# Reordering TensorE's products in a gated attention block: like divisions of the array side by side

## The chip, the core and the metric

The kernel runs on one core of one Trainium2 chip. Its time is the device time in microseconds (us) of one launch; the median of several runs is compared. All data are float32.

## What is computed

Two residual blocks over x (32 items of 256 tokens, 256 wide), cut to what matters:

```python
def _L0_xattn_ref(q, k, v, ...):        # k = v = ctx, 77 rows an item; H, D = 8, 128
    f_q, f_k, f_v = proj(q), proj(k), proj(v)   # layer_norm(t) @ w_in.T, split into 8 heads
    cosine_sim = einsum('hqnd,hqmd->hqnm', f_q, f_k) / (qn * kn)
    var_component = einsum('hqn,hqm->hqnm', q_ratio, k_ratio)
    cov_component = cosine_sim * decorr_scale       # one number a head, from all of f_q
    mixed = cw * cosine_sim + vw * cov_component + ww * var_component
    out = einsum('hqnm,hqmd->hqnd', mixed, f_v)
    return out_heads_side_by_side @ w_out.T + b_out

def _L0_ffn_ref(x, Wq, Wk, Wv, Wo, Wff):        # 16 heads of 16
    q, k, v = split_heads(x @ Wq), split_heads(x @ Wk), split_heads(x @ Wv)
    scores = einsum('bqd,bkd->bkq', q, k) / sqrt(256)
    z = einsum('bkq,bkv->bqv', softmax(scores, -1), v)
    z = l2_normalize(l2_normalize(z @ Wo) @ Wff)
    return gelu(z, approximate=False)

x = x + tanh(g_xattn) * _L0_xattn_ref(_layernorm(x), ctx, ctx, ...)
x = x + tanh(g_ffn) * _L0_ffn_ref(_layernorm(x), ...)
```

## The kernel before

A prologue (to about 150 us) loads and transposes the weights, gathers what the decorrelation scale needs from all tokens, and starts the first items. Then a software pipeline runs. Its unit is an item (256 tokens, two tiles of 128), and its order is written out by hand: the list `cycle` (line 1151) holds pairs of "how many items ahead" and a stage, and the loop at line 1216 runs through the list once a round, for n from -4 to 32. A round so holds stages of several items: the scores of item n, the output of item n-1, the attention of item n+1, the query features of n+2, the key features of n+3.

Each engine is wrapped in `InOrder` (line 22): its instructions stay in the order in which the stages issue them. So an instruction that waits holds up everything behind it on its engine. Semaphores between engines are set by the framework.

[...]Pool `ps` (line 71) has three tiles of one bank, called mm, which all products except two use: scores take two tiles of two banks (`ps_s`), the mix of values one bank (`ps_z`). A new mm tile goes to the bank that comes free first in the framework's planning; the product that writes it waits until the last reader of the bank's old tile is done.

TensorE's products differ in how they divide its 128 x 128 array:

- the whole array: query_features and key_features (`winT`, 512 columns of data), attend (`vw`,`s`), ff_project and ff_values, ff_out (`w_of`,`zT`), transpose_keys, the query ratios (`qrp`), and the transpositions against `ident` (xn, fq, xf);
- halves of 64 columns: `paired` (line 310), used by key_outputs and query_scores for pairs 0 and 1; two products side by side;
- quarters of 32 columns: pair 2 of key_outputs and query_scores, and mix_values (`zp`); four side by side;
- quarters of 32 rows: scores (`sc`).

A score unit u (0 to 3 in an item) is this chain: scores (line 491) makes four products on TensorE and two maxima on VectorE (`nm`, 1.2 us each); exponents (line 512), in two halves of four activations on ScalarE, with sums; scale_values (line 524) on VectorE takes the reciprocal of the sums and multiplies v into `vz`; mix_values (line 537) multiplies `vz` with the exponents on TensorE into `zp`. After unit 3, VectorE copies zp to `zT`.

ff_out (line 557) makes the two products of zT with `w_of`; ScalarE squares one half of the bank and VectorE copies the other to `u` after it. scale_queries (line 383) takes statistics of fq on VectorE, a power and the scaling of fq by `rq` on GpSimd. transpose_queries (line 398) transposes fq into `fqT`, copied out by ScalarE or VectorE. ff_add (line 602) adds u to x on VectorE and issues the output's DMA from SP. norm_inputs (line 194) makes `xn` on GpSimd; transpose_inputs (line 205) transposes it, and ScalarE copies it out with scale and bias as `xTc`. Every instruction is recorded under line 30, so the profile's groups are told apart by tile names.

Of the kernel before, what the change touches and what calls it, by code (L numbers as in the profile page):

```python
# [8 lines left out]
F32 = mybir.dt.float32  # L9
AF = mybir.ActivationFunctionType  # L10
ALU = mybir.AluOpType
# [3 lines left out]
P = 128  # L15
# [18 lines left out]
def gated_block_kernel(  # L34
# [25 lines left out]
    B, S, D = x.shape  # L60
    M = cx.shape[1]
    NT = S // P
# [6 lines left out]
    pa = ctx.enter_context(tc.tile_pool(name="pa", bufs=2))  # L69
# [6 lines left out]
    pe, act, dve, pool = (  # L76
        InOrder(tc, e) for e in (nc.tensor, nc.scalar, nc.vector, nc.gpsimd)
    )
# [8 lines left out]
    ident = const.tile([P, P], F32, name="ident")  # L87
# [11 lines left out]
    gcol = const.tile([P, 2], F32, name="gcol")  # L99
    bcol = const.tile([P, 2], F32, name="bcol")  # L100
# [36 lines left out]
    def mm_tile():  # L137
        return ps.tile([P, 512], F32, tag="mm", name="mm")
# [20 lines left out]
    def transpose_in(src):  # L159

        pt = mm_tile()
        for t in range(NT):
            for c in range(2):
                pe.transpose(
                    pt[:, c * S + t * P : c * S + (t + 1) * P],
                    src[:, t, c * P : (c + 1) * P],
                    ident,
                )
        return pt
# [6 lines left out]
    kept = [{} for _ in range(B)]  # L176
    given = set()

    def run(b, stage, *which):
        key = (b, stage.__name__, which)  # L180
        if key not in given:
            given.add(key)
            stage(b, *which)
# [21 lines left out]
    def transpose_inputs(b):  # L205
        k = kept[b]
        pt = transpose_in(k["xn"])
        xT = pa.tile([P, 2, S], F32, tag="xTc", name="xTc", bufs=1)
        for c in range(2):
            act.activation(  # L210
                xT[:, c, :], pt[:, c * S : (c + 1) * S], AF.Identity,
                bias=bcol[:, c : c + 1], scale=gcol[:, c : c + 1],
            )
        k["xTc"] = xT

# [94 lines left out]
    def paired(pt, k, pair, rhs):  # L310

        for c in range(2):
            for i in range(2):
                h = 4 * pair + 2 * c + i
                pe.matmul(
                    pt[MA * i : MA * (i + 1), c * S : (c + 1) * S],
                    lhsT=k["fvT"][:, h, 0:MA], rhs=rhs[:, h, :], start=True, stop=True,
                )

    def key_outputs(b, pair):  # L320


        k = kept[b]
        if pair == 0:
            k["vw"] = pa.tile([P, 5, D], F32, tag="vw", name="vw", bufs=2)
        pg = mm_tile()
        if pair < 2:
            paired(pg, k, pair, woutT)
            out = k["vw"][:, 2 * pair : 2 * pair + 2, :].rearrange("p g c -> p (g c)")
            (act.copy if pair == 0 else dve.tensor_copy)(out, pg)  # L330
            return
        for i in (1, 0):
            for j in range(4):
                n = 32 if i else MR + 1
                pe.matmul(
                    pg[32 * j : 32 * j + n, 0:D], lhsT=k["fvT"][:, 2 * j + i, MA : MA + n],
                    rhs=woutT[:, 2 * j + i, :], start=(i == 1), stop=(i == 0),
                )
        dve.tensor_tensor(k["vw"][:, 4, :], pg[:, 0:D], bias_t, ALU.add)

    def query_scores(b, pair):

        k = kept[b]
        if pair == 0:
            k["s"] = pa.tile([P, 5, S], F32, tag="s", name="s", bufs=1)
        pg = mm_tile()
        if pair < 2:
            paired(pg, k, pair, k["fqT"])
            out = k["s"][:, 2 * pair : 2 * pair + 2, :].rearrange("p g q -> p (g q)")
            (act.copy if pair == 0 else dve.tensor_copy)(out, pg)  # L350
            return
        for t in range(NT):
            pe.matmul(
                pg[:, t * P : (t + 1) * P], lhsT=qrps[t].rearrange("p h w -> p (h w)"),
                rhs=ident, start=(t == 0), stop=False,
            )
        for i in range(2):
            for j in range(4):
                n = MR + 16 * i
                pe.matmul(  # L360
                    pg[32 * j : 32 * j + n, 0:S], lhsT=k["fvT"][:, 2 * j + i, MA : MA + n],
                    rhs=k["fqT"][:, 2 * j + i, :], start=False, stop=(i == 1),
                )
        act.copy(k["s"][:, 4, :], pg[:, 0:S])
# [33 lines left out]
    def transpose_queries(b, t, hh):  # L398
        k = kept[b]
        if (t, hh) == (0, 0):  # L400
            k["fqT"] = pa.tile([P, H, S], F32, tag="fqT", name="fqT", bufs=1)
        pt = mm_tile()
        for i in range(4):
            h = hh * 4 + i
            pe.transpose(
                pt[:, i * P : (i + 1) * P], k["fq", t][:, h * P : (h + 1) * P], ident
            )
        out = k["fqT"][:, hh * 4 : hh * 4 + 4, t * P : (t + 1) * P]
        src = pt.rearrange("p (h q) -> p h q", q=P)
        (dve.tensor_copy if hh == t else act.copy)(out, src)  # L410

    def attend(b, t):

# [441 lines left out]
    qrps, vzs = [], []  # L855
# [55 lines left out]
    for g in range(-2, NG):  # L911
# [9 lines left out]
        for i in range(4):  # L921
            k = 4 * g + i
# [29 lines left out]
    pt = mm_tile()  # L952
# [7 lines left out]
    for c in range(2):  # L960
        dve.scalar_tensor_tensor(
            gs[:, c, c * P : D], gram[:, c, 0 : D - c * P], gcol[:, c : c + 1],
            grow[:, c * P : D], ALU.mult, ALU.mult,
        )
    run(0, transpose_inputs)
    run(1, norm_inputs)
    pt = mm_tile()
    for c in range(2):
        pe.matmul(
            pt[:, c * D + c * P : (c + 1) * D], lhsT=lbT[:, c * P : (c + 1) * P],  # L970
            rhs=lbT[:, D + c * P : 2 * D], start=True, stop=True,
# [11 lines left out]
    pt = mm_tile()  # L983
# [3 lines left out]
    pt = mm_tile()  # L987
    for h in range(H):
        for c in range(2):
            pe.matmul(  # L990
                pt[:, 2 * h : 2 * h + 2],
                lhsT=winT[:, c, h * P : (h + 1) * P],
                rhs=qk[:, c, :],
                start=(c == 0),
                stop=(c == 1),
# [21 lines left out]
    pt = mm_tile()  # L1017
# [20 lines left out]
    pt = mm_tile()  # L1038
# [6 lines left out]
    def square_up(hh):  # L1045
# [26 lines left out]
    pt = mm_tile()  # L1072
# [12 lines left out]
    pt = mm_tile()  # L1085
# [2 lines left out]
    dve.tensor_copy(ds, pt[0:H, 0:1])  # L1088
    pool.tensor_tensor(ds, ds, phalf, ALU.pow)
    act.activation(ds, ds, AF.Exp, scale=-5.0 / (P * P))  # L1090
    run(0, key_features)
    run(0, measure_keys)
    run(0, align_keys)
# [6 lines left out]
    dve.tensor_scalar(dg[:, 0, :], ident[0:H, 0:H], hw[:, 0:1], None, ALU.mult)  # L1100

    dve.tensor_scalar(dg[:, 1, :], ident[0:H, 0:H], lg[:, 2:3], 4.0, ALU.mult, ALU.mult)
    run(0, scale_queries, 1)
    run(0, transpose_queries, 0, 0)
    run(0, transpose_queries, 0, 1)
    pt = mm_tile()
    pe.matmul(
        pt[:, 0 : 2 * H], lhsT=ones[0:H, :], rhs=dg.rearrange("p w h -> p (w h)"),
        start=True, stop=True,
# [2 lines left out]

    run(0, weigh_keys)
    run(0, scale_keys)
    run(1, transpose_inputs)
    run(1, query_features, 0, 0)
    run(1, query_features, 0, 1)
    run(0, transpose_queries, 1, 0)
    run(0, transpose_queries, 1, 1)
    run(0, transpose_keys, 0)  # L1120
    run(0, transpose_keys, 1)
    run(1, key_features)
    for pair in range(3):
        run(0, query_scores, pair)
    for pair in range(3):
        run(0, key_outputs, pair)
    run(1, measure_keys)
    run(1, align_keys)
    run(0, attend, 0)
# [20 lines left out]

    cycle = [
        (4, load_queries),
        (0, ff_project, "k"),
        (0, ff_project, "q"),
        (0, ff_values),
        (1, transpose_queries, 0, 0),
        (-1, mix_values, 3),
        (1, transpose_queries, 0, 1),
        (0, scores, 0),
        (1, transpose_queries, 1, 0),  # L1160
        (1, transpose_queries, 1, 1),
        (0, exponents, 0, 0),
        (-1, ff_out, 0),
        (1, query_scores, 0),
        (-1, ff_out, 1),
        (1, query_scores, 1),
        (0, exponents, 0, 1),
        (0, scale_values, 0),
        (1, query_scores, 2),
        (-1, ff_norm_first),  # L1170
        (0, scores, 1),
        (-1, ff_norm_second),
        (2, transpose_inputs),
        (0, mix_values, 0),
        (2, measure_keys),
        (2, align_keys),
        (0, exponents, 1, 0),
        (0, exponents, 1, 1),
        (2, query_features, 0, 0),
        (2, query_features, 0, 1),  # L1180
        (0, scale_values, 1),
        (3, key_features),
        (2, weigh_keys),
        (0, scores, 2),
        (0, mix_values, 1),
        (2, scale_keys),
        (0, exponents, 2, 0),
        (1, attend, 0),
        (1, ff_stats, 0),
        (2, scale_queries, 0),  # L1190
# [7 lines left out]
        (2, query_features, 1, 0),  # L1198
        (2, query_features, 1, 1),
        (1, ff_norm, 1),  # L1200
        (2, transpose_keys, 0),
        (2, transpose_keys, 1),
        (0, scores, 3),
        (0, mix_values, 2),
        (-1, ff_add),
        (2, key_outputs, 0),
        (1, ff_transpose),
        (0, exponents, 3, 0),
        (2, key_outputs, 1),
        (0, exponents, 3, 1),  # L1210
        (2, key_outputs, 2),
        (2, scale_queries, 1),
        (0, scale_values, 3),
        (3, norm_inputs),
    ]
    for n in range(-4, B + 1):
        for ahead, stage, *which in cycle:
# [36 lines left out]
```

## Time and profile before

| what | value |
|---|---|
| time, median of 3 runs (lowest to highest) | 1516.35 us (1516.2 to 1518.54) |
| the profiled execution's own time | 1517.04 us |
| its span, first to last instruction | 1515.1 us |
| TensorE's mean granted clock | 0.982 |
| busy: DVE (VectorE), ACT (ScalarE), POOL (GpSimd) | 1044.1, 982.8, 516.8 us |
| busy: PEld (TensorE's weight loads, beside its products) | 846.5 us |
| a round of the cycle, between two zT copies | 42.26 us, in five rounds 43.98 us |
| first and last zT copy of the 32 items | 202.64 and 1499.91 us |
| HBM traffic over the span | 21 GB/s |

The longest waits are those of GpSimd for VectorE and ScalarE (`rq` 295.5 us, `i` 290.6 us, `rs` 230.0 us in total), of the VectorE maxima for the scores (115.2 us) and of ScalarE's `vw` copy for the products (107.4 us). Idle time of an engine that isn't the bottleneck costs nothing by itself.

How to read it: one execution was taken by the profiler. PE is TensorE's matmul stream; its ends are modelled, so times between starts are more exact than durations. In a line of a timeline stand the start, the time from there to the end of the last instruction merged into the line, the engine, the source line, the operation, out<-in by tile names, the shapes, and in brackets the idle time before it with what ended it.

### The profile page before, as it was taken

To read this page: it belongs to the slowest core of one execution; us is meant where nothing else is said; L and a number is where in the kernel's file an instruction comes from. 1 tells how busy PE (TensorE), PEld (TensorE's weight loads), DVE (VectorE), ACT (ScalarE), POOL (GpSimd) and SP (SyncE) were. 2 spreads that over 40 slices of the span, in tenths; PEclk is the share of its full clock that TensorE was granted. 3 is DMA by queue.
4 is the path that set the end of the run, shared out by engine and by line. 5 is a ranking of instruction groups with operands and counts; after the bars stand their busy time and mean duration, and the time that the engine had idled before them with its cause. 6 is when DMAs were issued, how large, how long until landed. Compare 5 with 4: busy or idle time off the path is not lost.

```text
span 1515.1 us, 26525 instructions
## 1 busy us (share of the span) xinstructions
PE 1468.9 (97%) x9313; PEld 846.5 (56%) x9313; DVE 1044.1 (69%) x2989; ACT 982.8 (65%) x3102; POOL 516.8 (34%) x656
## 2 busy tenths in 40 slices
PE   6898999999999999999999999999999999999985
PEld 6755555555555555555555555555555555555541
DVE  5735677777677676777676776776786767777843
ACT  5622566766676766766676766766676766766665
POOL 5912333333323323333323333333323323333311
PEclk9989999999999999999999999999999999999996
DMA  7500000000000000000000000000000000000000
GB/s 263 166 15 26 9 10 24 20 26 18 29 24 6 18 23 23 23 24 21 27 18 9 22 23 23 23 18 29 24 20 13 15 23 16 17 13 11 8 8 14
DMA packets 26194, 43.31 MB, mean 29 GB/s; under 512 B 6010, under 2 KB 11055, under 8 KB 26062
## 3 DMA queue, kind: packets, MB, share of 16 engines
q1 hardware_dynamic: 25230, 41.63, 8.6%
q8 instruction: 73, 1.20, 0.3%
q14 instruction: 59, 0.48, 0.1%
q10 hardware_dynamic: 832, 0.00, 0.0%
HBM read 22.98 MB, written 8.39 MB: 21 GB/s over the span
## 4 chain that ended last, share of the span: by engine, by line
PE 91%; ACT 2%; DVE 1%; POOL 0%; issue 0%; ACTq 0%; POOLq 0%
PE mm L30 73%; PE sc L30 9%; PE zp L30 8%; ACT e L30 1%; DVE nm L30 0%; ACT L30 0%; ACT ge L30 0%; POOL i L30 0%; POOL nrx L30 0%; DVE vz L30 0%; ACT fc L30 0%; DVE x L30 0%; ACT xT L30 0%; ACT xTc L30 0%; ACT u L30 0%
## 5 line engine op out<-in xcount | busy, mean ns | idle before, releaser
L30 ACT ACTIVATE e<-sc,nm 128x256 f32<-128x256 f32 x1024 | 469.8, 486 | 65.9 <-DVE nm L30 61.5
L30 DVE TENSOR_REDUCE nm<-sc 128x4 f32<-128x1024 f32 x256 | 301.4, 1218 | 115.2 <-PE sc L30 115.2
L30 PE MATMUL mm<-winT,xTc 128*128 128x512 f32 x512 | 235.6, 602 | 1.1 <-ACT xTc L30 1.1
L30 ACT ACTIVATION_READ_ACCUMULATOR e<-sc,nm 128x1 f32 x1024 | 224.1, 219 | 0.0
L30 POOL TENSOR_TENSOR rq<-qt,nhalf 128x8 f32<-128x8 f32 x64 | 105.4, 1647 | 295.5 <-DVE qt L30 295.5
L30 PE MATMUL sc<-q,kTf 32*128 32x512 f32 x1024 | 154.4, 648 | 6.1 <-ACT e L30 6.1
L30 PEld LDWEIGHTS mm<-winT,xTc 128*128 128x128 f32 x512 | 95.1, 191 | 107.3 <-issue 77.5
L30 PE MATMUL mm<-vw,s 128*128 128x256 f32 x640 | 147.7, 386 | 0.0
L30 PE MATMUL zp<-e,vz 128*32 128x256 f32 x2048 | 140.5, 393 | 5.1 <-DVE vz L30 5.1
L30 PEld LDWEIGHTS mm<-vw,s 128*128 128x128 f32 x640 | 119.6, 191 | 29.1 <-issue 14.1
L30 PE MATMUL mm<-w_of,zT 128*128 128x512 f32 x256 | 125.5, 614 | 0.8 <-DVE zT L30 0.8
L30 POOL TENSOR_TENSOR fq<-fq,rq 128x1024 f32<-128x1024 f32 x64 | 121.4, 1897 | 5.0
L30 POOL TENSOR_SCALAR i<-nn 128x2 f32<-128x2 f32 x64 | 14.3, 223 | 290.6 <-ACT ge L30 290.6
L30 PEld LDWEIGHTS zp<-e,vz 128*32 128x32 f32 x2048 | 54.3, 110 | 91.9 <-issue 33.9
L30 DVE BATCH_NORM_STATS2 qst<-fq 128x6 f32<-128x128 f32 x512 | 103.9, 275 | 0.0
L30 PE MATMUL mm<-fqT,fvT 128*64 128x256 f32 (+2 forms) x1024 | 102.9, 386 | 0.9 <-DVE fqT L30 0.7
L30 PE MATMUL mm<-woutT,fvT 128*64 128x256 f32 (+2 forms) x1024 | 101.0, 388 | 0.0
L30 POOL TENSOR_SCALAR rs<-mv 128x1 f32<-128x1 f32 x64 | 15.8, 247 | 231.5 <-DVE mv L30 230.0
L30 DVE COPY u<-mm 128x256 f32<-128x256 f32 x64 | 27.2, 425 | 91.5 <-ACT ge L30 91.4
L30 DVE TENSOR_TENSOR vz<-v,sums 128x128 f32<-128x128 f32 x128 | 86.8, 678 | 4.4
L30 ACT COPY fqT<-mm 128x512 f32<-128x512 f32 x64 | 37.5, 586 | 80.5 <-PE mm L30 80.5
L30 ACT COPY vw<-mm 128x512 f32<-128x512 f32 x32 | 18.8, 586 | 107.4 <-PE mm L30 107.4
(203 smaller groups left out, 2482.9 us busy)
## 6 DMA issues: line engine op xcount, KB each, us to landing
x<-in_x_dram SPq DMA_DIRECT2D x64, 256.0 KB
out_dram<-x SPq DMA_DIRECT2D x32, 256.0 KB
fv<-fvx SPq DMA_DIRECT2D x13, 308.0 KB
ct<-in_ctx_dram SPq DMA_DIRECT2D x4, 512.0 KB
w_in_n<-in_L_xattn_w_in_dram SPq DMA_DIRECT2D x2, 512.0 KB
w_out_n<-in_L_xattn_w_out_dram SPq DMA_DIRECT2D x1, 1024.0 KB
ct<-in_ctx_dram SPq DMA_DIRECT2D x1, 384.0 KB
fv<-fvx SPq DMA_DIRECT2D x1, 304.0 KB
```

The costliest lines, as they stand in the source:

```text
L30: return lambda *args, **kw: self._tc.keep_in_program_order(method(*args, **kw))
```

## The change

The list `cycle` is put into another order, and with it the stages of the first items ahead of it. In the new list each score unit stands beside products with 32 or 64 columns: the last mix and scores 0; scores 1, query_scores and mix 0; scores 2 and mix 1; scores 3, mix 2 and key_outputs. Between these four clusters stand stretches of whole-array products and transpositions. Projections k, q, v of an item and the first half of its queries' transposition go to the end of the round before; ff_add goes to the end of the round; norm_inputs goes ahead of transpose_keys.

To allow this, the query ratios, which were the first part of query_scores pair 2, become a stage of their own, query_ratios, whose mm tile is kept until pair 2 adds to it. key_outputs makes its `vw` tile at whichever pair comes first. The copy of xTc goes from ScalarE to VectorE. The copies of fqT are divided by half of the heads and no longer by half and tile: ScalarE takes heads 0 to 3, VectorE 4 to 7. No product, transposition or copy is added or left out.

```diff
@@ transpose_inputs
         for c in range(2):
-            act.activation(
-                xT[:, c, :], pt[:, c * S : (c + 1) * S], AF.Identity,
-                bias=bcol[:, c : c + 1], scale=gcol[:, c : c + 1],
+            dve.tensor_scalar(
+                xT[:, c, :], pt[:, c * S : (c + 1) * S], gcol[:, c : c + 1],
+                bcol[:, c : c + 1], ALU.mult, ALU.add,
             )
@@ key_outputs
-        if pair == 0:
+        if "vw" not in k:
             k["vw"] = pa.tile([P, 5, D], F32, tag="vw", name="vw", bufs=2)
@@
+    def query_ratios(b):
+
+        k = kept[b]
+        k["s"] = pa.tile([P, 5, S], F32, tag="s", name="s", bufs=1)
+        k["pr"] = mm_tile()
+        for t in range(NT):
+            pe.matmul(
+                k["pr"][:, t * P : (t + 1) * P], lhsT=qrps[t].rearrange("p h w -> p (h w)"),
+                rhs=ident, start=(t == 0), stop=False,
+            )
+
@@ query_scores
-        if pair == 0:
-            k["s"] = pa.tile([P, 5, S], F32, tag="s", name="s", bufs=1)
-        pg = mm_tile()
         if pair < 2:
+            pg = mm_tile()
             paired(pg, k, pair, k["fqT"])
...
-        for t in range(NT):
-            pe.matmul(
-                pg[:, t * P : (t + 1) * P], lhsT=qrps[t].rearrange("p h w -> p (h w)"),
-                rhs=ident, start=(t == 0), stop=False,
-            )
+        pg = k.pop("pr")
@@ transpose_queries
-        (dve.tensor_copy if hh == t else act.copy)(out, src)
+        (dve.tensor_copy if hh else act.copy)(out, src)
```

The order of the first items: transpose_inputs of item 1 goes ahead of key_features of item 0; scale_queries of item 0, tile 1, goes behind its scale_keys; key_outputs goes ahead of the query scores, in the order 2, 0, 1. The cycle after the change:

```python
cycle = [
    (4, load_queries),
    (-1, mix_values, 3), (0, scores, 0),
    (2, transpose_inputs), (0, exponents, 0, 0), (-1, ff_out, 0), (-1, ff_out, 1),
    (0, exponents, 0, 1), (1, transpose_queries, 1, 0), (1, transpose_queries, 1, 1),
    (2, query_features, 0, 0), (1, query_ratios), (0, scale_values, 0),
    (-1, ff_norm_first), (-1, ff_norm_second),
    (0, scores, 1), (1, query_scores, 0), (0, exponents, 1, 0), (1, query_scores, 1),
    (1, query_scores, 2), (0, exponents, 1, 1), (0, mix_values, 0),
    (2, measure_keys), (2, align_keys), (2, query_features, 0, 1), (0, scale_values, 1),
    (3, key_features), (2, weigh_keys),
    (0, scores, 2), (0, exponents, 2, 0), (0, mix_values, 1),
    (2, scale_keys), (1, attend, 0), (1, ff_stats, 0), (2, scale_queries, 0),
    (1, attend, 1), (0, exponents, 2, 1), (-1, ff_gelu), (2, warm_exponentials),
    (1, ff_norm, 0), (1, ff_stats, 1), (0, scale_values, 2),
    (2, query_features, 1, 0), (2, query_features, 1, 1), (1, ff_norm, 1),
    (3, norm_inputs), (2, transpose_keys, 0), (2, transpose_keys, 1),
    (0, scores, 3), (0, mix_values, 2),
    (2, key_outputs, 2), (2, key_outputs, 0), (2, key_outputs, 1),
    (1, ff_transpose), (2, transpose_queries, 0, 0), (0, exponents, 3, 0),
    (2, transpose_queries, 0, 1), (2, scale_queries, 1),
    (1, ff_project, "k"), (0, exponents, 3, 1), (1, ff_project, "q"), (1, ff_values),
    (0, scale_values, 3), (-1, ff_add),
]
```

## The prediction

> **What bounds the kernel now.** I read first the page's busy shares and its chain of waits, then the order of time on TensorE for one round of the main loop, then who waited for whom there.
>
> ```profile
> span 1515.1 us, 26525 instructions
> ...
> PE 1468.9 (97%) x9313; PEld 846.5 (56%) x9313; DVE 1044.1 (69%) x2989; ACT 982.8 (65%) x3102; POOL 516.8 (34%) x656
> ...
> PE 91%; ACT 2%; DVE 1%; POOL 0%; issue 0%; ACTq 0%; POOLq 0%
> ```
>
> TensorE is busy 97% of the span and holds 91% of the chain. Asked for TensorE's waits between 250 and 1390 us, the trace names none, and in the table by stretch PE is busy for all 1192.08 us from 202.64 to 1394.72 us. So in the steady rounds only TensorE's own time counts: what shortens its stream shortens the round, unless a new wait takes the place. A round is 42.26 us (zT copies start at 755.44 and 797.70), 43.98 in the five rounds that have two halves of key features.
>
> The stream itself, in order of time (start, duration, instructions; two matmul records per f32 product, one per transposition):
>
> ```profile
> 750.32 1.89 PE L30 MATMUL mm<-xT,w_q 128*128 128x256 f32 x8
> 752.05 1.89 PE L30 MATMUL mm<-w_v,xT 128*128 128x256 f32 x8
> 753.77 0.60 PE L30 MATMUL mm<-ident,fq 128*128 128x128 f32 x4
> 754.30 1.07 PE L30 MATMUL zp<-e,vz 128*32 128x256 f32 x16
> 755.31 0.66 PE L30 MATMUL mm<-ident,fq 128*128 128x128 f32 x4
> 755.89 1.14 PE L30 MATMUL sc<-q,kTf 32*128 32x512 f32 x8
> 756.97 1.09 PE L30 MATMUL mm<-ident,fq 128*128 128x128 f32 x8
> 757.89 1.88 PE L30 MATMUL mm<-w_of,zT 128*128 128x512 f32 x4
> 759.71 1.08 PE L30 MATMUL mm<-fqT,fvT 128*64 128x256 f32 x8
> 760.72 1.98 PE L30 MATMUL mm<-w_of,zT 128*128 128x512 f32 x4
> 762.64 1.08 PE L30 MATMUL mm<-fqT,fvT 128*64 128x256 f32 x8
> ```
>
> Ends are modelled here, so I go from start to start. Eight records of w_q take 1.73 us, 0.216 each: the undisturbed rate. w_of after whole-array work takes 1.82, between two 64-column blocks 1.92, so entering whole-array products costs 0.10. Four transpositions take 0.53 after whole-array work and 0.58 after zp (entry 0.05), eight take 0.92, so 0.11 each, and 0.53 - 0.44 = 0.09 is the exit. A 64-column block has four rounds of 0.216 = 0.86 and takes 1.01; zp the same 0.86 and 1.01; sc 0.86 and 1.08. With the exit of 0.09 taken off, and about 0.02 because the four tiles start staggered, the entries are 0.05 (64 columns), 0.03 (32 columns), 0.10 (scores).
>
> **What the Trainium skill says.** "TensorEngine Tiling (Array Packing)", Key Properties: changing the tiling mode, and not only the tile, drains TensorE. The trace agrees and prices it: 0.09 at each change, whichever way. "TensorE: Matmul & The Clock Gate", LDWEIGHTS (loading the stationary operand): a load takes its columns over 1.2 GHz, so 0.107 us for 128 columns, 0.053 for 64, 0.027 for 32. My entries of 0.10, 0.05 and 0.03 are just that: the first load after a change isn't hidden. (The transpositions' 0.05 is less, and I use the measured value.) "SBUF — State Buffer", Who interferes with whom: a VectorE instruction with two SBUF inputs contends with a GpSimd instruction that reads SBUF, and who issues first blocks the other. The trace agrees: scale_values' product (vz) takes 0.29 us alone and 1.94 when GpSimd's scaling of fq has begun before it.
>
> ```profile
> 751.94 0.19 DVE L30 RECIPROCAL sums<-sums 128x8 f32<-128x8 f32 x1
> 752.16 0.29 DVE L30 TENSOR_TENSOR vz<-v,sums 128x128 f32<-128x128 f32 x1
> ...
> 783.34 1.94 DVE L30 TENSOR_TENSOR vz<-v,sums 128x128 f32<-128x128 f32 x1
> ```
>
> ```profile
> 751.58 1.65 POOL L30 TENSOR_TENSOR rq<-qt,nhalf 128x8 f32<-128x8 f32 x1 [7.81 <-DVE qt L30]
> 753.30 1.90 POOL L30 TENSOR_TENSOR fq<-fq,rq 128x1024 f32<-128x1024 f32 x1
> ...
> 783.24 1.90 POOL L30 TENSOR_TENSOR fq<-fq,rq 128x1024 f32<-128x1024 f32 x1
> ```
>
> **The change part by part.**
>
> *Mode changes.* No product is added or taken away. In the old cycle a round enters whole-array products 5 times, transpositions 4, scores 4, 64 columns 4, 32 columns 6: 23 changes. In the new one it is 2, 2, 4, 2 and 4: 14. Nine drains of 0.09 are 0.8; the entries saved are 3 x 0.10 + 2 x 0.05 + 2 x 0.05 + 2 x 0.03 = 0.56. Sum: 1.4 us a round.
>
> *Transpositions of xn and output products, now back to back.* Four banks must come free in a row, with three in the pool. In the built program query_features(2,0,0) takes the bank of the second ff_out and waits for its u copy. That runs: 0.21 from the end of the products to ScalarE's start (v's products end at 753.77, the copy starts at 753.98), 0.47 for square and accumulator read, 0.42 for the copy, some 0.05 to be seen: 1.15. Meanwhile TensorE has eight transpositions, 0.88. With a first load of 0.10 that can't be pulled ahead, it stands still for 0.4 us. Bounds: 0 (if loads are still pulled ahead and copies are quick) to 0.6.
>
> *query_ratios* keeps a bank until query_scores 2. The program gives it the bank of the transposition that VectorE empties, free about 1.5 us before it is asked for; query_scores 0 and 1 take banks that ScalarE empties while the score unit runs. Cost 0; without that cover up to 0.5.
>
> *xTc on VectorE.* Two tensor_scalar from PSUM, not in the trace on VectorE; nearest rows 0.41 (xf) and 0.48 (x from mm): 0.45 each, 0.9 a round. They run after the score maxima (2.27 us for the pair), while ScalarE computes the first exponents (0.45 each, 1.80 for a unit's half). Their successors, the u copies, wait for ScalarE anyway. ScalarE is freed of 1.0. Cost 0; if VectorE were late, at most 0.9.
>
> *fqT's copies.* Those of (0,0) and (0,1) change engines with each other, 0.59 on ScalarE for 0.69 on VectorE; the load of neither changes, and their place is in the next part.
>
> *The last mix.* The tightest place. Let X be the end of transpose_queries(2,0,0) on TensorE. ScalarE: its copy from X + 0.25 (behind xT's), exponents 3,0 from X + 0.74 to 2.54, kTf copy to 3.05, exponents 3,1 to 4.85, last accumulator read to 5.0. VectorE: reciprocal X + 5.04, vz 5.27 to 5.56. TensorE: transpositions 0.44, k, q and v 3 x 1.73, drain 0.09: X + 5.72. No wait, with 0.1 to spare. The scores behind it need the q copies, done by X + 6.1, and are due at X + 6.6.
>
> *scale_queries(2,1), ff_add, norm_inputs.* VectorE copies fqT from X + 0.64 and starts the statistics at X + 1.25; GpSimd's scaling of fq starts 4.33 later in the trace (748.97 to 753.30), so at X + 5.58. vz starts 0.3 before it and isn't blocked. ff_add (0.74, two SBUF inputs) follows vz directly: I take it that it goes first and GpSimd waits. Its output DMA comes later, and its place among eight x buffers is far from needed. norm_inputs on GpSimd (2.47) goes ahead of the power and scaling of scale_queries(2,1), but falls into some six idle us (7.81 in the row above). SP's load and align queue keeps its order. Cost 0.
>
> *Before and after the loop.* Moved steps of the first items, one switch less: -1 us (0 to -4). In the last three rounds (40.8, 36.4 and 28.0 us) TensorE waits for exponents, and I charge them as one full round together.
>
> Sum: (1.4 - 0.4) x 29 rounds = 29, and 1: 30 us. The profiled execution took 1517.0 (span 1515.1 and 1.9 around it), 0.7 above the median, so 1487.
>
> **The rivals.**
>
> - *GpSimd takes the port before ff_add.* It asks at X + 5.58, when vz has just ended or is ending; my times are not good to 0.1. Then ff_add ends at X + 8.2 and zT's copy, due at X + 6.8, at 8.8. The output products wait 0.6, the wait above stays: 0.4 a round gained, 12 + 1 us: about 1504. For it: the margin. Against it: ff_add is next in VectorE's queue.
> - *Slower: vz behind GpSimd's scaling.* If exponents 3,1 end 0.3 later than I have them, vz starts after X + 5.58, takes 1.94 as at 783.34 and ends at X + 7.8, and the last mix stands still for 2.1 a round, the scores and all else behind it. 1.4 - 0.4 - 2.1 = -1.1, times 29: about 1548. It decides at vz's start against the scaling's start. Against it: the chains hang on the same transpositions, and ScalarE's steps have measured spacings.
> - *No new wait.* All 1.4 x 29 = 41 are kept: about 1475. Against it: 1.15 is longer than 0.88.
> - *The change doesn't do what it says.* The built order has the 14 changes, so this is left only as waits elsewhere that eat the gain: about 1500 to 1517.
>
> **How the numbers follow.** Forecast 0.45, GpSimd first 0.25, no wait 0.10, waits elsewhere 0.07, vz blocked 0.13. The range takes in the first three and the bounds of the 0.4 (0 to 0.6): 1472 to 1510. Within 0.2%, 3 us, about what a measurement of this kernel can tell from no change: 0.03, out of the waits elsewhere. Slower 0.13, faster 0.84.
>
> **What would show it.** After: rounds of about 41.3 us; 14 changes, each with 0.09 and its entry; a single TensorE wait in a round, before winT<-xTc, for DVE u; 0.29 for the last vz; x<-u at 0.74. If x<-u shows 2.5 or more, the first rival holds; if two of four vz in a round take 1.9 and zp waits for vz, the second. I'm wrong if drains stay at 0.09 a change but rounds aren't shorter by what is counted, or if TensorE waits for ScalarE in other places.

## The result and the profile after

| | before | after |
|---|---|---|
| median (lowest to highest), us | 1516.78 (1516.2 to 1518.54, 4 runs) | 1493.71 (1491.96 to 1499.29, 4 runs) |
| ratio, with 95% interval | | 0.9852 [0.9824, 0.988] |
| profiled execution, and its span | 1517.04, 1515.1 | 1491.96, 1490.2 |
| TensorE's mean granted clock | 0.982 | 0.983 |
| a round, and a round with two halves of key features | 42.26, 43.98 | 41.50, 43.21 |
| first zT copy | 202.64 | 203.91 |
| from there to the 29th zT copy (28 rounds) | 1192.08 | 1170.85 |
| from the 29th zT copy to the end | 120.40 | 115.39 |

The change makes the kernel 1.5% faster. The forecast was 1487; the median lies 6.7 above it, inside the range of 1472 to 1510. The profiled execution of after is its fastest run, 1.75 below the median; the sums here are made against it. The last three rows of the table, taken together, are the whole difference in span: +1.3 - 21.2 - 5.0 = -24.9.

The page of after, the same three lines as before: span, busy times, chain of waits.

```profile
span 1490.2 us, 26481 instructions
...
PE 1439.0 (97%) x9313; PEld 863.3 (58%) x9313; DVE 1078.1 (72%) x3053; ACT 938.0 (63%) x3038; POOL 531.1 (36%) x656
...
PE 88%; ACT 3%; DVE 3%; issue 1%; POOL 0%; ACTq 0%; POOLq 0%
```

TensorE has the same 9313 matmuls in 29.9 us less busy time, and is still the bound. But the chain now goes through VectorE and ScalarE a little more (6% instead of 3%): TensorE waits for them where it didn't before. The waits of TensorE in the steady part (250 to 1370 us), which named nothing before, show one line of 10 waits:

```profile
PE mm L30 <- DVE u L30: 1.5, 10, 0.2
```

That view understates it: a wait is only counted from the modelled end of the instruction before. Start-to-start times in TensorE's order of time are better. The first half of this fence holds the stretch that begins with the transpositions of xn, the second the output products of the keys:

```profile
747.75 0.66 PE L30 MATMUL mm<-ident,xn 128*128 128x128 f32 x4
748.24 3.60 PE L30 MATMUL mm<-w_of,zT 128*128 128x512 f32 x8
751.67 1.04 PE L30 MATMUL mm<-ident,fq 128*128 128x128 f32 x8
752.86 1.98 PE L30 MATMUL mm<-winT,xTc 128*128 128x512 f32 x4 [0.15 <-DVE u L30]
754.68 0.61 PE L30 MATMUL mm<-ident,qrp 128*128 128x128 f32 x4
...
776.50 1.07 PE L30 MATMUL zp<-e,vz 128*32 128x256 f32 x16
777.38 3.15 PE L30 MATMUL mm<-woutT,fvT 128*32 128x256 f32 x32
780.47 0.66 PE L30 MATMUL mm<-ident,xf 128*128 128x128 f32 x4
```

First: w_of's eight records, split by 64-column blocks before, now take 3.43 in one piece, 8 x 0.429, with no entry and no drain inside. Second: from the start of the eight fq transpositions to winT's first product are 1.19 us, though they need 0.88; winT's four then take 1.82 instead of 1.72. That is the forecast wait for the u copy's bank, and the first load that can't be pulled ahead behind it: 0.31 + 0.10. The view of TensorE's weight loads (PEld) has that load starting together with its product, after the u copy:

```profile
752.86 0.30 PEld L30 LDWEIGHTS mm<-winT,xTc 128*128 128x128 f32 x2 [0.39 <-DVE u L30]
```

Third: the woutT block takes 3.09 (777.38 to 780.47). It was not expected to wait; without a wait it needs 2.86 (774.85 to 777.71 in run 3; 2.85 in run 1, shown below), so 0.23 are lost.

Around the last mix, VectorE's and GpSimd's order of time:

```profile
745.15 0.29 DVE L30 TENSOR_TENSOR vz<-v,sums 128x128 f32<-128x128 f32 x1
745.36 0.74 DVE L30 SCALAR_TENSOR_TENSOR x<-u,tg,x 128x512 f32<-128x512 f32 x1
```

```profile
745.50 2.36 POOL L30 TENSOR_TENSOR fq<-fq,rq 128x1024 f32<-128x1024 f32 x1
```

vz takes its undisturbed 0.29, ff_add its 0.74, and GpSimd's scaling, issued 0.14 after ff_add, takes 2.36 instead of 1.90. ff_add went first, as forecast, and the other engine paid.

Now the stretch in which the woutT block loses 0.23:

```profile
776.42 0.66 DVE L30 TENSOR_SCALAR xf<-x,mv,rs 128x256 f32<-128x256 f32 x1 [0.18 <-POOL rs L30]
777.00 0.54 DVE L30 COPY fvT<-mm 128x384 f32<-128x384 f32 x1
```

```profile
776.37 2.47 POOL L30 TENSOR_SCALAR xn<-x,mv_x,rstd_x 128x256 f32<-128x256 f32 x2
```

The second xf (x normalized for the feed-forward block, made on VectorE) takes 0.66 here and 0.41 before (786.06). It starts 0.05 after GpSimd has begun norm_inputs (xn), which the change put just there. The fvT copy (what transpose_keys has made), next in VectorE's order, comes 0.25 later for it, and key_outputs pair 2, the first in the woutT block, needs fvT. So far this is read from one trace; runs 1 and 8 test it.

### The profile page after: what moved, and what is told of

Its sections match the earlier page's. It is cut to its first block, busy times and chain, and to the rows that moved or that the text cites. A ratio compares the mean times of both kernels' runs of the same rounds, so it can differ in the third digit from the quotient of the medians.

```text
span 1490.2 us, 26481 instructions
## 1 busy us (share of the span) xinstructions
PE 1439.0 (97%) x9313; PEld 863.3 (58%) x9313; DVE 1078.1 (72%) x3053; ACT 938.0 (63%) x3038; POOL 531.1 (36%) x656
## 4 chain that ended last, share of the span: by engine, by line
PE 88%; ACT 3%; DVE 3%; issue 1%; POOL 0%; ACTq 0%; POOLq 0%
PE mm L30 70%; PE sc L30 9%; PE zp L30 8%; ACT e L30 2%; ACT ge L30 1%; DVE u L30 1%; DVE nm L30 1%; ACT L30 0%; DVE kst L30 0%; DVE kt L30 0%; POOL i L30 0%; DVE vz L30 0%; POOL nrx L30 0%; DVE xTc L30 0%; ACT u L30 0%
## 5 line engine op out<-in xcount | busy, mean ns | idle before, releaser
L30 PE MATMUL mm<-winT,xTc 128*128 128x512 f32 x512 | 243.8, 608 | 6.4 <-DVE xTc L30 2.2
L30 ACT ACTIVATION_READ_ACCUMULATOR e<-sc,nm 128x1 f32 x1024 | 227.8, 222 | 0.0
L30 POOL TENSOR_TENSOR fq<-fq,rq 128x1024 f32<-128x1024 f32 x64 | 135.0, 2109 | 5.0
L30 PE MATMUL mm<-w_of,zT 128*128 128x512 f32 x256 | 117.9, 604 | 0.8 <-DVE zT L30 0.8
L30 PEld LDWEIGHTS zp<-e,vz 128*32 128x32 f32 x2048 | 57.4, 110 | 95.5 <-issue 33.3
L30 PE MATMUL mm<-fqT,fvT 128*64 128x256 f32 (+2 forms) x1024 | 93.9, 383 | 0.0
L30 POOL TENSOR_SCALAR xn<-x,mv_x,rstd_x 128x256 f32<-128x256 f32 x64 | 79.1, 1248 | 10.3 <-issue 10.3
```

The lines of the kernel that those rows point to most:

```text
L30: return lambda *args, **kw: self._tc.keep_in_program_order(method(*args, **kw))
```

## The experiments

The theory: the changes of division saved 1.4 a round as priced, and two waits gave part of it back, the u copy's (0.41) and a missed one that norm_inputs causes through VectorE (0.23). The rivals: the price of a change is wrong (smaller), the moved ff_add or xTc set the round, or it is an effect of run and clock. The round, between zT copies, is the measure; three kernels with the same cycle (runs 3, 9 and 12) agree on 40.86. The first items do not: in the profiled runs of this study the first zT copy lies between 202 and 218 us. Each time stands beside runs of the kernel before on the same chip, so ratios are compared.

| run | round, us | first zT | median, us | ratio to before |
|---|---|---|---|---|
| after | 41.50 | 203.91 | 1493.71 | 0.9852 [0.9824, 0.988] |
| 1 norm_inputs early | 41.28 | 208.16 | 1489.31 | 0.9818 [0.9805, 0.983] |
| 2 features between | 41.10 | 209.95 | 1487.32 | 0.9799 [0.9787, 0.9812] |
| 3 both | 40.86 | 209.82 | 1479.96 | 0.9751 [0.9739, 0.9764] |
| 4 two changes more | 41.78 | 210.80 | 1507.39 | 0.9927 [0.9913, 0.9942] |
| 5 statistics early | 41.97 | 209.35 | 1511.36 | 0.9958 [0.9941, 0.9974] |
| 6 mix 1 late | 41.51 | 209.53 | 1496.64 | 0.9866 [0.9849, 0.9882] |
| 7 ff_add back | 41.89 | 210.76 | 1507.11 | 0.9937 [0.9922, 0.9952] |
| 8 before, norm_inputs late | 42.26 | 202.19 | 1517.51 | 1.0002 [0.9993, 1.0011] |
| 9 both, first items a | 40.86 | 217.55 | 1486.63 | 0.9794 [0.978, 0.9809] |
| 10 both, xTc on ScalarE | 41.01 | 207.18 | 1480.66 | 0.9761 [0.9747, 0.9776] |
| 11 both, mix 1 late | 41.06 | 207.50 | 1483.41 | 0.9785 [0.977, 0.9799] |
| 12 both, first items b | 40.86 | 210.94 | 1478.57 | 0.9745 [0.9729, 0.9762] |

**1. norm_inputs early.** The kernel after, with one step moved:

```diff
         (3, key_features),
+        (3, norm_inputs),
         (2, weigh_keys),
...
         (1, ff_norm, 1),
-        (3, norm_inputs),
```

> The changed kernel with norm_inputs moved ahead of weigh_keys, so that GpSimd makes xn some 13 us earlier in the round. Theory: in the changed kernel xn starts on GpSimd just as VectorE starts the second xf, xf takes 0.66 instead of 0.41 us, the fvT copy behind it is late, and key_outputs 2 stands still for 0.23 us a round. Then here xf is back at 0.41, that block at 0.67 us from first to last start instead of 0.89, the round at 41.27 us instead of 41.50, the time 6 to 7 us lower. Rival (the fvT copy is late for another reason, such as the score maxima or the blocked vz ahead of it): xf or not, the round stays at 41.50.

The round fell by 0.22. TensorE's order of time, and then VectorE's, in this kernel:

```profile
778.73 2.92 PE L30 MATMUL mm<-woutT,fvT 128*32 128x256 f32 x32
781.58 0.66 PE L30 MATMUL mm<-ident,xf 128*128 128x128 f32 x4
```

```profile
777.77 0.41 DVE L30 TENSOR_SCALAR xf<-x,mv,rs 128x256 f32<-128x256 f32 x1 [0.18 <-POOL rs L30]
778.10 0.55 DVE L30 COPY fvT<-mm 128x384 f32<-128x384 f32 x1
```

xf is back at 0.41, the woutT block at 2.85. The missed wait was norm_inputs' doing.

**2. Features between.** query_features(2,0,0) is put between the two transpositions, so that it takes a bank which is free by then:

```diff
-        (1, transpose_queries, 1, 0),
         (1, transpose_queries, 1, 1),
         (2, query_features, 0, 0),
+        (1, transpose_queries, 1, 0),
```

> The changed kernel with query_features(2,0,0) put between the two groups of query transpositions, tile 1's second half first. It then takes the bank of the first output product, whose u copy is done 0.2 us before, and the last transpositions take the bank of the second one. Theory: TensorE's wait for the second u copy, 0.31 us a round with the load that it lays bare, goes and nothing takes its place: round 41.19 us instead of 41.50, 9 us off the time. Rival (the wait only moves to the next bank, that of the last transpositions or of query_ratios): round within 0.05 of 41.50.

The round fell by 0.40 instead of 0.31. The expectation had counted only the later start of winT; the 0.10 of the load that isn't hidden came back too. TensorE's order of time in run 3, which has this edit as well, and then its first weight load for winT, which starts 0.11 ahead of its product:

```profile
749.55 0.60 PE L30 MATMUL mm<-ident,fq 128*128 128x128 f32 x4
749.99 1.88 PE L30 MATMUL mm<-winT,xTc 128*128 128x512 f32 x4
751.71 0.60 PE L30 MATMUL mm<-ident,fq 128*128 128x128 f32 x4
752.15 0.61 PE L30 MATMUL mm<-ident,qrp 128*128 128x128 f32 x4
```

```profile
749.88 0.30 PEld L30 LDWEIGHTS mm<-winT,xTc 128*128 128x128 f32 x2
```

0.44 + 1.72 + 0.44 = 2.60 from fq to qrp, where after has 3.01: the wait cost 0.41.

**3. Both edits.**

> Both moves at once: norm_inputs early, and query_features between the transpositions. Theory: the two waits are separate and TensorE has no other of weight: round 40.96 us, 15 to 16 us below the changed kernel, about 1477. Rival (one chain is behind both): the gain is that of the better one alone.

The round is 40.86, that is 1.40 under the kernel before, with the 14 changes of the kernel after. With both waits gone, all of the worked-out 1.4 is there. The expectation was 0.10 short of that, since it took the wait for the u copy at 0.31, as run 2's did. This version beats both kernels: 0.9751.

**4. Two changes more.** The price by itself, the other way round: ff_transpose, whole-array work, is put into the 64-column stretch.

```diff
         (2, key_outputs, 0),
-        (2, key_outputs, 1),
         (1, ff_transpose),
+        (2, key_outputs, 1),
```

> The changed kernel with ff_transpose put back between key_outputs 0 and 1, as it stood before: two more changes of the array's division, nothing else. Theory (each change costs a drain of 0.09 and the first load of what follows, 0.055 for transpositions, 0.05 for 64 columns): 0.29 us a round more, less 0.07 if the wait of the k projection for the xT copy goes: round 41.72 to 41.79, 6 to 8 us slower. Rival (the changed kernel is faster by its other waits and engines, and changes cost nothing that isn't hidden): round 41.43 to 41.50.

The round grew by 0.28. The prices give two drains of 0.09 and the entries of transpositions (0.05) and 64 columns (0.05): 0.28. In the trace the stretch from woutT to the k projection grew by 0.31 (4.76, from 787.88 to 792.64, instead of 4.45), and the k projection behind it takes 1.76 instead of 1.80, so the price holds to about 0.03. The time grew by more than the 28 x 0.28 = 8 of the rounds; this kernel's first zT copy came 6.9 later than after's, which run 12 below takes up.

**5. Statistics early.** Is the slower rival (vz behind GpSimd's scaling) real? Here the statistics start without the fqT copy ahead of them, so GpSimd comes first.

```diff
-        (2, transpose_queries, 0, 1),
         (2, scale_queries, 1),
+        (2, transpose_queries, 0, 1),
```

> The changed kernel with scale_queries(2,1) ahead of transpose_queries(2,0,1), so that GpSimd's scaling of fq starts about 1.5 us earlier in the round, before the last vz and not after it. This makes the slower rival of the prediction happen on purpose. Theory (who issues first keeps the shared port for its whole instruction): the last vz of a round lasts from its start to about 0.1 after the scaling's end, 0.9 us instead of 0.29; the last mix waits 0.45; round 41.95 us, 12 to 13 us slower than the changed kernel, about 1506. Rival (TensorE's wait comes from ScalarE's chain and not from the port): vz at 0.29, round 41.50.

VectorE, GpSimd and TensorE in this kernel, each in its order of time:

```profile
756.24 0.94 DVE L30 TENSOR_TENSOR vz<-v,sums 128x128 f32<-128x128 f32 x1
757.10 0.74 DVE L30 SCALAR_TENSOR_TENSOR x<-u,tg,x 128x512 f32<-128x512 f32 x1
```

```profile
755.13 1.90 POOL L30 TENSOR_TENSOR fq<-fq,rq 128x1024 f32<-128x1024 f32 x1
```

```profile
757.23 1.07 PE L30 MATMUL zp<-e,vz 128*32 128x256 f32 x16 [0.40 <-DVE vz L30]
```

The scaling, issued 1.11 before vz, keeps its 1.90; vz takes 0.94, to 0.15 behind the scaling's end, and the last mix waits 0.40. The round is 0.47 longer. So the mechanism exists, and the order of issue decides it. Its price is smaller than the 2.1 that the prediction's rival put on it, since vz comes when much of the scaling is done.

**6 and 11. Mix 1 late.** One change more, in the middle of a whole-array stretch; in 6 on the kernel after, in 11 on the version of run 3.

```diff
-        (0, mix_values, 1),
         (2, scale_keys),
         (1, attend, 0),
+        (0, mix_values, 1),
```

> The changed kernel with mix 1 moved from behind scores 2 to between the two attend groups: scores, whole array, 32 columns, whole array in place of scores, 32 columns, whole array. One change of division more, and no chain that hangs on it. Theory (a drain of 0.09 and 0.10 for the first whole-array load): 0.19 us a round more, 41.69, 5 to 6 us slower. Rival (a change among cut arrays, scores to 32 columns, costs as much as two changes by way of the whole array, or the load is hidden): round 41.50 to 41.60.

Run 6 missed: the round stayed as it was (41.51). Its woutT block took 2.88 (783.29 to 786.17) instead of 3.09, and the products from scores 2 to the end of attend took 0.20 more. The reading was that the change does cost 0.20 where it stands, and that the later wait for fvT, which hangs on VectorE and not on TensorE, shrinks by the same. In run 11 that wait is gone beforehand.

> The kernel after with norm_inputs and query_features moved as in the run with both edits, and mix 1 put between the two attend groups. That is one change of the array's division more, and it cuts the whole-array stretch. In the run with mix 1 late alone, the added change cost 0.20 us where it stood, but the output products of the keys waited 0.20 less later, and the round stayed as it was. Here that later wait is gone beforehand. Theory (a change costs what was priced, and was only swallowed by the wait): the round grows by 0.20 from 40.86 to 41.06, and the time by about 5.6 over the run with both edits, 1485 to 1486. Rival (the change costs nothing, mix 1 finds its place for free): round 40.86, time 1480.

Run 11 has the 0.20: 41.06 against 40.86. TensorE's order of time there:

```profile
761.36 1.14 PE L30 MATMUL sc<-q,kTf 32*128 32x512 f32 x8
762.43 2.42 PE L30 MATMUL mm<-vw,s 128*128 128x256 f32 x10
764.78 1.07 PE L30 MATMUL zp<-e,vz 128*32 128x256 f32 x16
765.78 2.43 PE L30 MATMUL mm<-vw,s 128*128 128x256 f32 x10
768.05 3.60 PE L30 MATMUL mm<-winT,xTc 128*128 128x512 f32 x8
```

From sc to winT are 6.69 us; in after the same products take 6.49 (763.65 to 770.14). The time rose by 0.34% of before (0.9785 against 0.9751), 5.2 us, for 28 x 0.20 = 5.6.

**7. ff_add back** behind mix 2, on the kernel after.

```diff
         (0, mix_values, 2),
+        (-1, ff_add),
...
         (0, scale_values, 3),
-        (-1, ff_add),
```

> The kernel after with ff_add back behind mix 2, where it stood before the change. Theory (the move to the end of the round was needed, because there VectorE is waiting anyway): ff_add's 0.74 on VectorE now stands ahead of the addition that empties the bank of key_outputs 2, which ff_transpose takes; that has some 0.2 to spare, so TensorE waits about 0.5 before the transposition of xf: round 41.85 to 42.05 instead of 41.50, time 10 to 15 above the kernel after, and GpSimd's scaling of fq at the end of the round takes 1.90 instead of 2.36. Rival (VectorE has slack there): round 41.50, the same time.

The round is 0.39 longer: ff_transpose waits for the bank of key_outputs 2. TensorE there, and then VectorE in the next round:

```profile
747.40 3.14 PE L30 MATMUL mm<-woutT,fvT 128*32 128x256 f32 x32
750.87 0.66 PE L30 MATMUL mm<-ident,xf 128*128 128x128 f32 x4 [0.32 <-DVE vw L30]
```

```profile
791.63 0.73 DVE L30 SCALAR_TENSOR_TENSOR x<-u,tg,x 128x512 f32<-128x512 f32 x1
```

ff_add stands between the score maxima and the addition into vw that empties that bank, so the bank comes free later. Its move to the end of the round was needed in the new order, though it makes GpSimd's scaling longer there (2.36 in after, 1.90 here).

**8. Before, with norm_inputs late.** Does the contention come only with the new order? In the kernel before, norm_inputs is moved ahead of transpose_keys.

```diff
+        (3, norm_inputs),
         (2, transpose_keys, 0),
...
-        (3, norm_inputs),
     ]
```

> The kernel before with one edit: norm_inputs at the place that it has in the changed kernel, ahead of transpose_keys. Theory: the second xf of a round then meets xn on GpSimd and takes 0.66 instead of 0.41 us here too; no product asks for the fvT copy so early in the old order, so the round stays at 42.26 us and the time at that of before. Rival (xf's longer time belongs to something else of the new order): xf 0.41.

VectorE and GpSimd, in their orders of time:

```profile
743.35 0.66 DVE L30 TENSOR_SCALAR xf<-x,mv,rs 128x256 f32<-128x256 f32 x1 [0.18 <-POOL rs L30]
```

```profile
743.30 2.47 POOL L30 TENSOR_SCALAR xn<-x,mv_x,rstd_x 128x256 f32<-128x256 f32 x2
```

xf takes the same 0.66, and neither round nor time moves. In the old order 64-column products and transpositions stand ahead of key_outputs 2; there VectorE has the time. The same contention costs nothing in one order and 0.23 in the other.

**9. First items a.** On run 3's version, norm_inputs of item 2 goes ahead of ff_transpose of item 0, its transpose_inputs behind ff_values, and item 1's second query_features group ahead of item 0's transpose_keys.

```diff
     run(1, query_features, 0, 0)
+    run(1, query_features, 0, 1)
     run(0, transpose_keys, 0)
     run(0, transpose_keys, 1)
-    run(1, query_features, 0, 1)
...
+    run(2, norm_inputs)
     run(0, ff_transpose)
...
     run(0, ff_values)
+    run(2, transpose_inputs)
```

> Both moves that help the changed kernel (norm_inputs early, query_features between the transpositions) and two edits ahead of the loop: item 1's second query_features group goes ahead of item 0's transpose_keys, and item 2's xn is made and transposed before the loop begins. Theory: in the first 210 us TensorE waits for dk and for xTc, and its granted clock falls to 0.57 to 0.85 in some 10 us after such waits; with the waits filled the first zT copy comes at 203 to 205 us instead of 208 to 210, rounds stay at 40.86: about 1474, 4 to 6 us below both moves alone. Rival (the first items' time has another cause): first zT copy at 208 to 210, time as with both moves.

It had the opposite effect: GpSimd was late with xn, and TensorE's order of time shows

```profile
165.80 0.69 PE L30 MATMUL mm<-ident,xn 128*128 128x128 f32 x2 [6.96 <-POOL xn L30]
```

The granted clock of the stretch from 155 to 170 us is 0.77. The first zT copy is 7.7 later than in run 3.

**10. xTc back on ScalarE**, on run 3's version (the two copies as before the change).

> The kernel after with both edits, and the two copies of xTc back on ScalarE, as they were before the change. Forecast at cost 0 and without a gain of its own: the u copies wait for ScalarE's squares anyway. Theory (the move to VectorE made no difference to the round): round 40.86 to 40.96, time 0 to 3 above the run with both edits. Rival (the move was needed, since ScalarE's squares of ff_out come 1.0 later behind the copies and TensorE waits for the u copy's bank): 0.5 or more a round, 41.36 or above, time 1494 or above.

The round is 41.01, 0.15 longer, and just outside what the theory gave. winT's first product starts 0.05 later behind the transpositions, and its four take 1.82 instead of 1.72, as in the wait for the u copy: it is that wait again, 0.05 + 0.10, for the first u copy this time (which ends at 749.00; winT starts at 749.06). In time the two can't be told apart (0.9761 [0.9747, 0.9776] against 0.9751): the 28 rounds are 3.9 longer together, but the first zT copy comes 2.6 earlier. There the copies on ScalarE help. In the first items VectorE has the score maxima in front of the xTc copies, and TensorE waits; first run 3, then run 10:

```profile
170.72 3.43 PE L30 MATMUL mm<-winT,xTc 128*128 128x512 f32 x4 [1.87 <-DVE xTc L30]
```

```profile
168.48 1.98 PE L30 MATMUL mm<-winT,xTc 128*128 128x512 f32 x4 [0.22 <-ACT xTc L30]
```

So the move of xTc to VectorE was not free: it costs a wait once, in front of the first score units (1.98 in after), and saves one in each round of run 3's order.

**12. First items b.** norm_inputs of item 2 earlier still, and query_features left where run 3 has it.

```diff
     run(1, transpose_inputs)
+    run(2, norm_inputs)
     run(0, key_features)
...
     run(0, ff_values)
+    run(2, transpose_inputs)
```

> The kernel after with both edits, and in the first items norm_inputs of item 2 right behind transpose_inputs of item 1, where GpSimd has little to do, and transpose_inputs of item 2 behind ff_values of item 0. The steady rounds stay as they are: 40.86. Theory (TensorE's wait of 1.98 for the copy of xTc in front of the first score units can be had away, and it is GpSimd's late xn that made the earlier try dear): no wait of 7 us for xn, none of 2 us for xTc; the first zT copy 2 to 4 us earlier than 209.8, and the time 2 to 4 below the run with both edits, 1476 to 1478. Rival (the time of the first items is set by the clock granted after idle stretches, not by this wait): the wait goes and the first zT copy stays at 209 to 211.

The 1.87 before winT (run 3) became 0.52 + 0.30 + 0.29 in three places. The first zT copy wasn't earlier, but this run was 3.3 us late before the edit could act: its products of the same work took longer between 90 and 103 us. The table by stretch of run 3, then of run 12 (PE, PEld, DVE, ACT, POOL busy; clock; DMA):

```profile
97.00:103.40 6.40, 6.40 (x16) 2.66 (x14) 2.70 (x8) 0.59 (x1) 0.80 (x2) 1.00 0.00 0
```

```profile
97.00:103.40 6.40, 6.40 (x14) 2.54 (x12) 0.95 (x4) 0.58 (x1) 0.80 (x2) 0.62 0.00 0
```

Products of the same order, clock 1.00 and 0.62. Counted from the product that waits for VectorE's dg (122.04 and 125.36), run 12 needs 85.6 to the first zT copy and run 3 87.8. Half of these 2.2 us have already arisen when woutT's products start (134.09 and 136.34), ahead of the products that the edit moves, while the clock from 125 to 135 us is 0.71 in run 12 and 0.57 in run 3. In time the difference (0.9745 and 0.9751) is within the intervals, so a gain is likely and not shown.

## Why the prediction was right, and where it was off

- *Changes of division, 1.4 a round: right.* With its rounded prices the sum is 0.81 + 0.56 = 1.37. Run 3, with the same 14 changes and both waits gone, gives 1.40; run 4 gives 0.28 for two changes priced at 0.28, and run 11 gives 0.20 for one priced at 0.19. What the Trainium skill says in "TensorEngine Tiling (Array Packing)", Key Properties, that changing the mode drains TensorE, holds; the price, here 0.09 and an entry of 0.03 to 0.10, comes from the traces. One reading doesn't follow from the lines shown: both the 64-column block and zp take 1.01, which leaves 0.04 as the entry of either. The starts of single products in the trace of before tell them apart: the first step of a block takes 0.266 instead of 0.216 with 64 columns (at 759.71) and 0.240 with 32 (at 754.31), so entries of 0.05 and 0.02, near the 0.053 and 0.027 that the prediction estimated from the skill's figure.
- *The wait for the second u copy, 0.4: right.* The lines of after and run 3 give 0.41 and run 2's round 0.40, in the place and for the reason that were named.
- *norm_inputs "falls into some six idle us ... Cost 0": the failed step.* It asked only whether GpSimd has time, and not who runs on VectorE meanwhile. It cost 0.23 a round, 28 x 0.23 = 6.4 us. 1.40 - 0.41 - 0.23 = 0.76 is what the round of after gained. The warning was to be had: the Trainium skill, "SBUF — State Buffer", Who interferes with whom, which the prediction drew on for vz, says as well that tensor_scalar can enter a mode that takes the port shared with GpSimd, if its operands meet that mode's conditions, and that the later of the two instructions is then blocked for the whole of the first. The trace agrees that xf is slowed; but xf ended after 0.66, while the first of the two xn runs to about 1.2 (half of 2.47). So it was not held up for the whole of the other instruction, as vz is, and whether it is that mode isn't shown. Runs 1 and 8 show that xf takes 0.66 where xn has begun just before it, and 0.41 where it hasn't.
- *The k projection* takes 1.80 instead of 1.73 behind the transpositions, 0.07 a round, in after and in run 3 alike. The old order paid an entry of 0.10 in that place, which the 1.37 counts as saved; 0.03 of it was. The other terms must then be some 0.1 low together, spread over nine drains and nine entries that are given to 0.01. A late xT copy may be part of the 0.07: it ends at 781.75 in after, 0.08 before k starts. In run 4 it ends more than 1 us before, and k takes 1.76; the other 0.03 stays open.
- *query_ratios 0, last mix no wait, ff_add first: right.* vz takes 0.29 and ff_add 0.74, and TensorE waits for neither. GpSimd's 2.36 delays nothing that TensorE waits for.
- *xTc on VectorE, 0 and at most 0.9: right for the steady rounds of after, wrong ahead of them.* The copies do run after the score maxima, as the prediction says; in the first items winT needs them at once and waits 1.98 for them, which run 10 brings down to 0.22 by moving them back.
- *The edges.* Forecast -1 for the first items and -1 for the last three rounds; measured +1.3 and -5.0. The +1.3 contains the wait of 1.98 for xTc. Nearly all of the -5.0 is in the one round that starts at 1435.5 before: 31.96 instead of 36.43. TensorE's order of time there, before and then after:

```profile
1446.38 1.07 PE L30 MATMUL zp<-e,vz 128*32 128x256 f32 x16
1449.73 1.57 PE L30 MATMUL sc<-q,kTf 32*128 32x512 f32 x4 [2.28 <-ACT e L30]
1451.56 2.08 PE L30 MATMUL sc<-q,kTf 32*128 32x512 f32 x4 [0.25 <-ACT e L30]
1453.56 1.94 PE L30 MATMUL zp<-e,vz 128*32 128x256 f32 x16
1455.43 5.40 PE L30 MATMUL mm<-vw,s 128*128 128x256 f32 x20
```

```profile
1428.39 1.13 PE L30 MATMUL sc<-q,kTf 32*128 32x512 f32 x4 [0.85 <-ACT e L30]
1429.44 1.07 PE L30 MATMUL zp<-e,vz 128*32 128x256 f32 x16
1430.44 4.58 PE L30 MATMUL mm<-vw,s 128*128 128x256 f32 x20
```

Before, a wait of 2.28 is followed by products that take up to twice their time (zp 1.87 from start to start, for 1.00), at a mean clock of 0.91 over the round; after, the wait is 0.85 and the clock stays at 1.00. I had priced the waits of the last rounds, but not the clock behind them. It isn't chance of one execution: this round takes 36.43 in the profiles of before and of run 8, which have the old order, and 31.95 to 32.16 in all others.

Summed: forecast -28 for 28 rounds, -1 and -1; measured -21.2, +1.3 and -5.0. The missed wait is most of the 6.8 that the rounds fell short, and the unforeseen 4 of the last rounds hid more than half of it. That the median came within 7 us of the forecast is in part luck: an error in the rounds and one at the end had opposite signs. Of the rivals, "no new wait" (1475) is what run 3 comes near: it keeps all of the 1.4 and has 1479.96, with its first items later than after's.

What stays open is why the first zT copy of nearly all variants of after lies at 207 to 211 and that of its own profiled run at 203.9. The clock granted between 125 and 135 us is 0.99 there and 0.57 in run 3, and behind nearly the same wait for xTc (1.98 and 1.87) winT's four take 1.79 there and 3.22 in run 3; which of it belongs to the kernel and which to the run isn't settled.

## What to carry to other kernels

Where TensorE is the bound, count the changes of how its array is divided and price each from start-to-start times in the trace; here the sum came out within 0.03 of 1.40 us a round, and putting like products together was worth it. For every step that is moved, ask not only whether its own engine is free but what runs meanwhile on the engine that it can slow, and what is queued behind that; and ask it for the first items too, where the neighbours are others than in the steady rounds. A cost that has no effect in one order, or a gain that a later wait swallows, has to be tested on a version in which that wait is gone.

## What the runs showed of the hardware

- A VectorE tensor_scalar with one SBUF tensor (xf) takes 0.66 instead of 0.41 us when GpSimd's tensor_scalar has begun 0.05 before it; ff_add, begun 0.14 before GpSimd's scaling, stays at 0.74 and makes the scaling 2.36 instead of 1.90.
- When TensorE had to wait for a bank, the load of its next product wasn't pulled ahead: it started with the product (752.86 in after) and not 0.11 before it (run 3), and the wait of 0.31 cost 0.41.
- After waits of some 2 us the same products ran at up to twice their time (zp 1.87 for 1.00; in run 1 winT's four 3.38 for 1.79 behind a wait of 1.98). It isn't so each time: in after the same wait of 1.98 is followed by 1.79.
